# Judging an attention's unshifted exps behind it instead of checking norms in front of it

## The chip, the cores and the metric

The kernel runs on one core of one Trainium2 chip. A core has five engines, each with an instruction queue of its own: TensorE (PE; its weight loads are listed as PEld), VectorE (DVE), ScalarE (ACT), GpSimd (POOL) and SyncE (SP), and 16 DMA engines. The metric is the device time of one execution in microseconds (us): the median of several runs.

## The reference, cut to what matters

Two layers follow each other on 2304 tokens (48 x 48) of 256 channels, all in 32-bit floats. Layer 0 is the one that the change is about: a group norm, three projections, and an attention in which every token contributes 4 rows of 64 channels, so 9216 queries meet 9216 keys.

```python
q = xt @ Wq.T + bq; k = xt @ Wk.T + bk; v = xt @ Wv.T + bv
qf = q.reshape(B * H * W * nh, dk) / jnp.sqrt(jnp.float32(dk))
kf = k.reshape(B * H * W * nh, dk)
vf = v.reshape(B * H * W * nh, dv)
A = jax.nn.softmax(qf @ kf.T, axis=1)
O = A @ vf
out = O.reshape(B, H, W, nh * dv) @ Wo.T + bo      # and x = x + out
```

Layer 1 is an attention over 64 learnt slices of the tokens and a mixture of 8 experts, of which each token uses two.

A softmax is safe in floating point when the largest score of a row is subtracted ahead of the exponential. Without that it gives the same result as long as no sum of exponentials overflows or vanishes. The inputs are normal random numbers, and q and k come from normalised rows and weights of standard deviation 1/16.

## The kernel before, in words

The whole kernel is one function, `tile_conv_attn_hybrid_kernel`, written out as one straight program. A framework (Tile) assigns buffers, inserts semaphores, and orders the instructions of each engine. Instructions issued through `nc.tensor`, `nc.vector` and so on may be reordered by it; those issued through `pe`, `dve`, `act` and `pool` (class `InOrder`, line 55 is what the profile names for all of them) keep the order in which they are written.

**Projections** (lines 235 to 389). After the group norm, a loop over five blocks of tokens (four of 512, one of 256; line 281) makes q and k: for each half m of the channels two matmuls into a PSUM tile `pq` (line 294) and two into `pk` (line 298). Both have the name `pp` and take turns in four buffers of the pool `ps_pj`. From `pq`, VectorE writes three copies and ScalarE one into q2 (lines 312 and 316), from `pk` ScalarE writes kk (line 321).

**The check in front.** Each block also squares q and k on ScalarE (lines 303 and 322), sums the squares per head on TensorE with a matrix `hsel` of zeros and ones (line 328, tile `pn`), and takes maxima on VectorE (line 331). Behind the blocks one transpose (line 338) and a few tiny instructions make `ok`: one if the largest norm of q times the largest norm of k is at most 40, so that no score can be larger than that. Then v follows, 18 tiles of 128 tokens (line 347), again in `pp`, and some folded weights (lines 364 to 389).

**The fork.** `ok` is loaded into a register of each engine (line 674), and `tc.If` (line 677) takes `attention(False)` or, in its Else, `attention(True)`. The latter finds each query's largest score first (`largest`) and adds its negative to the scores by another matmul.

**The attention** (line 503) has 18 blocks of 512 queries; in each a loop over 36 pairs of key tiles. For a pair, `scores` makes 8 score matmuls into `s`, ScalarE takes the exponential into `p` (5 buffers), VectorE adds `p` to `acc` (`sums`), and `times_values` multiplies by v into `av`, one pair behind. The block's end work is spread over the next block: `close` folds `acc` to `both` and `av` to `up`; `between` (at pair 1) sums `both` over the partitions by a matmul of ones into `pb`, and returns a list of small pieces of work: `invert` (reciprocal of the sums), `divide`, and the pieces of `follow`, which runs the output projection, the layer norm and the slice weights of earlier tokens. Each piece has a rank; `in_turn` sorts by it, and one piece is done per pair (`later.pop(0)()`, line 651). In the last block four more rounds of `follow` are drained in the same way (lines 652 to 657). The tiles `pa` and `pb` exist once each.

**Behind the attention** come the last tokens, the slice attention, the gates and the routing. The routing makes 43 slots of 128 token rows, each with one expert (lines 900 to 1030); `slot_t` holds the token numbers, with which GpSimd gathers rows. The loop over the slots (from line 1115) does, for slot s: load slot s + 2, `first(s)` (32 weight loads and matmuls into `ph`, ScalarE's Gelu), and `second(s - 1)` (matmuls into `py`, VectorE's two instructions for `y`, GpSimd's scatter with addition into `t_d`). The last part reads `t_d`, transposes it, and writes the output by SyncE (lines 1132 to 1146). The end of the program (line 1177) waits for the last transfer and clears the semaphores.

Of the kernel before, what the change touches and what calls it, by code (L numbers as in the profile page):

```python
# [14 lines left out]
P = 128  # L15
C = 256
NT = 2304
# [7 lines left out]
NPAIR = NF // (2 * P)  # L25
SAFE = 40.0
S = 64
# [32 lines left out]
@with_exitstack  # L60
def kernel(
    ctx: ExitStack,
    tc: tile.TileContext,
    x, Wq, bq, Wk, bk, Wv, bv, Wo, bo,
    W0, b0, Ws, bs, Wqkv, bqkv, Wout, bout,
    Wg, bg, W1, b1, W2, b2,
    out,
):
    nc = tc.nc
    x_v = x[0].rearrange("(c p) h w -> p c (h w)", p=P)  # L70
# [156 lines left out]
    WoT = l0.tile([P, 2, C], FP, name="WoT")  # L227
    hsel = l0.tile([P, 32], FP, name="hsel")
    hv = hsel.rearrange("p (a b) -> p a b", b=2)
    nc.vector.memset(hsel, 0.0)  # L230
    nc.vector.memset(hv[0:DK, :, 0], 1.0)
    nc.vector.memset(hv[DK:P, :, 1], 1.0)
    ok = l0.tile([1, 1], mybir.dt.int32, name="ok")

    with proj, tc.tile_pool(name="sq", bufs=2) as sqp, tc.tile_pool(
        name="ps_pj", bufs=4, space=PSUM
    ) as ps_pj, tc.tile_pool(name="ps_w", bufs=2, space=PSUM) as ps_w, tc.tile_pool(
        name="ps_n", bufs=1, space=PSUM
    ) as ps_n:
        def transposed(dst, raw):  # L240
# [38 lines left out]

        nmx = pj.tile([P, len(TBLOCKS)], FP, name="nmx")  # L280
        for bi, (t0, tn) in enumerate(TBLOCKS):
            toks = slice(t0, t0 + tn)
            for c in range(2):
# [3 lines left out]
                )  # L287
            sqs = []
            for m in range(2):
                cols = slice(m * P, (m + 1) * P)  # L290
                pq = ps_pj.tile([P, 512], FP, name="pp", tag="pp")
                pk = ps_pj.tile([P, 512], FP, name="pp", tag="pp")
                for c in range(2):
                    nc.tensor.matmul(  # L294
                        pq[:, 0:tn], WqT[:, c, cols], xn[:, c, toks], start=(c == 0), stop=(c == 1)
                    )
                for c in range(2):
                    nc.tensor.matmul(  # L298
                        pk[:, 0:tn], WkT[:, c, cols], xn[:, c, toks], start=(c == 0), stop=(c == 1)
                    )  # L300
                sq = sqp.tile([P, 2, 512], FP, name="sq", tag=f"sq{m}")
                sqs.append(sq)
                nc.scalar.activation(  # L303
                    sq[:, 0, 0:tn], pq[:, 0:tn], AF.Square, bias=bq8[:, m : m + 1], scale=0.125
                )
                for j in range(2):
                    rows = slice(j * DK, (j + 1) * DK)
                    at = (2 * m + j) * NT + t0
                    for half in range(2):
                        dst = q2[half * DK : (half + 1) * DK, at : at + tn]  # L310
                        if j == 1 and half == 1:
                            nc.scalar.activation(
                                dst, pq[rows, 0:tn], AF.Identity, bias=bq8[rows, m : m + 1], scale=0.125
                            )
                        else:
                            nc.vector.tensor_scalar(  # L316
                                dst, pq[rows, 0:tn], bcol[rows, B_Q + m : B_Q + m + 1], 0.125,
                                ALU.add, ALU.mult,
                            )
                bk_m = bcol[:, B_K + m : B_K + m + 1]  # L320
                nc.scalar.activation(kk[:, m, toks], pk[:, 0:tn], AF.Identity, bias=bk_m)
                nc.scalar.activation(sq[:, 1, 0:tn], pk[:, 0:tn], AF.Square, bias=bk_m)

            pn = ps_n.tile([P, 512], FP, name="pn", tag="pn")
            for kind in range(2):
                for m in range(2):
                    r = (2 * kind + m) * 32
                    nc.tensor.matmul(  # L328
                        pn[r : r + 32, 0:tn], hsel, sqs[m][:, kind, 0:tn], start=True, stop=True
                    )  # L330
            nc.vector.tensor_reduce(nmx[:, bi : bi + 1], pn[:, 0:tn], AX.X, ALU.max)
            if bi == 0:
                WvT = transposed(pj.tile([P, 2, C], FP, name="WvT"), raws["Wv"])
                transposed(WoT, raws["Wo"])
        nm = pj.tile([P, 1], FP, name="nm")
        nc.vector.tensor_reduce(nm, nmx, AX.X, ALU.max)
        pr = ps_n.tile([1, P], FP, name="pr", tag="pn")
        nc.tensor.transpose(pr, nm, ident)
        qk2 = pj.tile([1, 2], FP, name="qk2")
        nc.vector.tensor_reduce(qk2, pr.rearrange("p (a b) -> p a b", a=2), AX.X, ALU.max)  # L340
        top = pj.tile([1, 1], FP, name="top")
        nc.vector.tensor_mul(top, qk2[:, 0:1], qk2[:, 1:2])
        nc.vector.tensor_scalar(ok, top, SAFE * SAFE, None, ALU.is_le)
        for i in range(NTT):
# [43 lines left out]
        nc.vector.tensor_copy(bout_bc[:, C : C + E], pw[:, 208:216])  # L388
        nc.vector.tensor_copy(cs_bc, pw[:, 216:224])


# [110 lines left out]

    def attention(shifted):


        with tc.tile_pool(name="pexp", bufs=5) as pexp, tc.tile_pool(
# [107 lines left out]
            def between(b, st):  # L614
# [16 lines left out]

                work.extend([(0, invert), (1, divide)])
                return in_turn(work)
# [4 lines left out]
            for b in range(NQB):  # L638
                row = largest(b) if shifted else None
                st = {}  # L640
                for pair in range(NPAIR):
# [10 lines left out]
                    elif b == NQB - 1 and pair < NPAIR - 1 and drained < 4:  # L652
# [3 lines left out]
                        drained += 1  # L656
                        later.pop(0)()

# [7 lines left out]
            lower()  # L666
            invert, divide = between(NQB - 1, behind)
            invert()
            halves()
            divide()  # L670

    small_scores = nc.values_load(
        ok, min_val=0, max_val=1, skip_runtime_bounds_check_because="it is the result of a comparison"
    )
    with tc.If(small_scores > 0) as fork:
        attention(False)
    with fork.Else():
        attention(True)  # L680

# [219 lines left out]
    with gating, tc.tile_pool(name="onehot", bufs=1) as oh, tc.tile_pool(  # L901
# [125 lines left out]
        dve.tensor_scalar(empties, pw[:, 0, :], 0.0, spare, ALU.is_equal, ALU.mult)  # L1027
        dve.scalar_tensor_tensor(slot_t, pw[:, 0, :], -1.0, empties, ALU.add, ALU.add)
        dve.tensor_copy(slot_w, pw[:, 1, :])
# [7 lines left out]
    with tc.tile_pool(name="ps_h", bufs=3, space=PSUM) as ps_h, tc.tile_pool(  # L1037
        name="ps_y", bufs=2, space=PSUM
    ) as ps_y, tc.tile_pool(name="ps_t", bufs=2, space=PSUM) as ps_t:

# [69 lines left out]
        def turn_next(s):  # L1110
            if s < NSL:
                xs, w1 = loaded.pop(s)
                turned[s] = turn(xs), w1

        turn_next(0)
        for s in range(NSL):
# [3 lines left out]
            if s == 0:  # L1120
                turn_next(1)
            else:
                second(s - 1, hid.pop(s - 1), lambda: turn_next(s + 1))
        second(NSL - 1, hid.pop(NSL - 1), lambda: None)


    with tc.tile_pool(name="fin", bufs=3) as fin, tc.tile_pool(
        name="ps_f", bufs=4, space=PSUM
    ) as ps_f:
        for t0, n in TBLOCKS:  # L1130
# [5 lines left out]
            for c in range(2):  # L1136
# [7 lines left out]
                else:  # L1144
                    nc.scalar.copy(ob[:, c, 0:n], pt[:, 0:n])
            nc.sync.dma_start(out=out_v[:, :, t0 : t0 + n], in_=ob[:, :, 0:n])


# [33 lines left out]
```

## Time and profile before

| what | value |
|---|---|
| median of 3 runs | 1681.72 us (1681.07 to 1682.72) |
| the profiled execution | 1684.09 us |
| its span, first to last instruction | 1682.3 us |
| mean granted clock of TensorE | 0.971 |
| projections, 15.52 to 61.21 us | TensorE busy 45.67 of 45.69 |
| v and folded weights, 61.21 to 79.10 us | TensorE busy 17.89 of 17.89 |
| attention, 79.10 to 1254.70 us | TensorE busy 1170.3 of 1175.6, VectorE 890.87, ScalarE 683.5 |
| slice attention and routing, 1254.7 to 1339.4 us | TensorE busy 56.59 of 84.7 |
| expert slots, 1339.4 to 1656.0 us | TensorE busy 314.99 of 316.6 |
| the rest, 1656.0 to 1682.3 us | TensorE busy 7.51 of 26.3 |

The page of a profile gives, for one execution, the busy time of each engine, the span cut into 40 slices with the busy tenths of each engine and the clock that TensorE was granted, the chain of work that ended last, and the costliest groups of instructions. From the trace behind it one can ask for a timeline, for one tile's or one line's instructions, for the waits, and for a table of busy times by stretch. A matmul of 32-bit floats counts as two instructions. Times within the span are counted from its first instruction.

### The profile page before, as it was taken

What the parts mean: (1) busy time and instruction counts of PE and PEld (TensorE: products, weight loads), DVE (VectorE), ACT (ScalarE), POOL (GpSimd) and SP (SyncE); (2) the same over time, 40 slices, a digit from 0 to 9 for tenths busy, and PEclk for the clock granted to TensorE, in tenths of its full rate; (3) what the DMA queues carried; (4) which work ended last, traced back from release to release, by engine and by line L of the source; (5) the groups of instructions that cost most, each with busy time, mean ns of one, the idle gap of its engine ahead of it and who ended that gap; (6) DMA issues with size and microseconds to landing.
All of it is one profiled execution on the core that took longest, in us unless ns stands there. A gap on an engine that the chain in (4) does not pass through costs nothing.

```text
span 1682.3 us, 32323 instructions
## 1 busy us (share of the span) xinstructions
PE 1617.2 (96%) x13416; PEld 824.3 (49%) x13416; DVE 1039.0 (62%) x1340; ACT 831.7 (49%) x1152; POOL 157.5 (9%) x133
## 2 busy tenths in 40 slices
PE   7999999999999999999999999999987599999995
PEld 3633343333333333333333333333445599999994
DVE  6577777777777777776876877777775511111111
ACT  4355565555655555655655655555542233333331
POOL 0000000000000000000000000000001333333331
PEclk9999999999999999999999999999996599999997
DMA  4000000000000000000000000000007366666664
GB/s 132 1 1 1 1 1 1 1 1 1 1 1 1 1 1 2 1 2 1 2 1 2 2 1 1 1 1 1 1 4 262 135 185 185 188 179 176 183 182 125
DMA packets 41266, 82.91 MB, mean 49 GB/s; under 512 B 3693, under 2 KB 26810, under 8 KB 40986
## 3 DMA queue, kind: packets, MB, share of 16 engines
q1 hardware_dynamic: 32858, 69.49, 12.6%
q0 software_dynamic: 8256, 11.28, 3.9%
q8 instruction: 109, 1.79, 0.5%
q14 instruction: 43, 0.35, 0.1%
HBM read 67.78 MB, written 12.98 MB: 48 GB/s over the span
## 4 chain that ended last, share of the span: by engine, by line
PE 75%; issue 12%; POOL 6%; DVE 3%; DMA 3%; ACT 0%; POOLq 0%; SPq 0%; DVEq 0%; ACTq 0%
PE s L55 33%; PE av L55 33%; POOL t_d L1101 3%; POOL xs L1044 3%; PE pa L55 2%; PE pb L55 1%; DMA t_d<-y,slot_t 1%; PE pp L294 1%; PE pw L55 1%; PE pp L347 1%; PE pp L298 1%; PE pn L328 1%; DMA tt<-t_d 0%; DVE s L55 0%; DMA Wq_raw<-in_L_conv_Wq_dram 0%
## 5 line engine op out<-in xcount | busy, mean ns | idle before, releaser
L55 DVE TENSOR_TENSOR acc<-acc,p 128x1024 f32<-128x1024 f32 x612 | 748.1, 1222 | 270.7 <-ACT p L55 264.2
L55 ACT ACTIVATE p<-s 128x1024 f32<-128x1024 f32 x648 | 663.0, 1023 | 495.8 <-PE s L55 485.7
L55 PE MATMUL av<-p,v_sb 64*64 64x512 f32 x5184 | 676.4, 590 | 1.0 <-DVE up L55 0.7
L55 PE MATMUL s<-q,kk 64*64 64x512 f32 x5184 | 676.0, 590 | 0.0
L55 PEld LDWEIGHTS s<-q,kk 64*64 64x64 f32 x5184 | 202.2, 133 | 351.9 <-issue 180.7
L55 PEld LDWEIGHTS av<-p,v_sb 64*64 64x64 f32 x5184 | 195.9, 131 | 358.0 <-ACT p L55 207.2
L55 ACT ACTIVATE hid<-ph,bcol 128x128 f32<-128x128 f32 x344 | 98.2, 367 | 237.7 <-PE ph L55 198.2
L55 PEld LDWEIGHTS ph<-xT,w 128*128 128x128 f32 x1376 | 163.0, 195 | 3.1 <-DVE xT L55 0.9
L55 PE MATMUL ph<-xT,w 128*128 128x128 f32 x1376 | 163.3, 278 | 0.5 <-DVE xT L55 0.5
L55 PE MATMUL py<-w_sb,hid 128*128 x688 | 162.4, 379 | 0.0
L55 POOL TENSOR_TENSOR rstd_t<-ve,mhalf 128x1 f32<-128x1 f32 (+1 forms) x21 | 28.5, 1356 | 1262.1 <-DVE ve L55 1262.1
L55 DVE COPY xT<-pt 128x256 f32<-128x256 f32 x43 | 18.3, 425 | 186.6 <-PE pt L55 186.6
L55 PEld LDWEIGHTS py<-w_sb,hid 128*128 128x128 f32 x688 | 124.2, 190 | 13.4
L1101 POOL DMA_INDIRECT t_d<-y,slot_t x43 | 68.2, 1585 | 96.2 <-DVE y L55 93.3
L55 DVE TENSOR_TENSOR y<-py,b_bc 128x256 f32<-128x256 f32 x43 | 18.3, 425 | 80.0 <-PE py L55 80.0
L1044 POOL DMA_INDIRECT xs<-tn_d,slot_t x43 | 45.8, 1065 | 120.3 <-PE pt L55 106.9
L55 DVE RECIPROCAL rinv<-pb 128x256 f32<-128x256 f32 x18 | 31.5, 1751 | 0.0
L55 DVE TENSOR_TENSOR acc<-p 128x1024 f32<-128x1024 f32 x18 | 22.1, 1225 | 9.3 <-ACT p L55 9.3
L316 DVE TENSOR_SCALAR q<-pp,bcol 64x512 f32<-64x512 f32 (+1 forms) x30 | 20.8, 694 | 11.2 <-ACT sq L303 10.8
L1139 PE MATMUL pt<-ident,tt 128*128 128x128 f32 x36 | 7.5, 390 | 16.2 <-DMA tt<-t_d 16.2
L55 PE MATMUL pw<-what,t_sb 128*128 128x86 f32 x72 | 15.7, 422 | 6.7 <-POOL what L55 6.7
L55 DVE TENSOR_REDUCE up<-av 128x512 f32<-128x1024 f32 x18 | 21.9, 1217 | 0.0
(252 smaller groups left out, 628.0 us busy)
## 6 DMA issues: line engine op xcount, KB each, us to landing
w<-in_L_ffn_W_dram SPq DMA_DIRECT2D x43, 1024.0 KB
w_sb<-in_L_ffn_W_dram SPq DMA_DIRECT2D x8, 1024.0 KB
x_sb<-in_x_dram SPq DMA_DIRECT2D x4, 576.0 KB
t_d<-t_sb SPq DMA_DIRECT2D x3, 768.0 KB
tn_d<-tn SPq DMA_DIRECT2D x3, 768.0 KB
tt<-t_d SPq DMA_DIRECT2D x4, 512.0 KB
out_dram<-ob SPq DMA_DIRECT2D x4, 512.0 KB
b_bc<-in_L_ffn_b_dram SPq DMA_DIRECT2D x1, 1024.0 KB
```

Source lines behind the costliest of these rows:

```text
L55: return self.tc.keep_in_program_order(getattr(self.engine, name)(*args, **kwargs))
L294: nc.tensor.matmul(pq[:, 0:tn], WqT[:, c, cols], xn[:, c, toks], start=(c == 0), stop=(c == 1))
L298: nc.tensor.matmul(pk[:, 0:tn], WkT[:, c, cols], xn[:, c, toks], start=(c == 0), stop=(c == 1))
L316: nc.vector.tensor_scalar(dst, pq[rows, 0:tn], bcol[rows, B_Q + m : B_Q + m + 1], 0.125, ALU.add, ALU.mult,)
L328: nc.tensor.matmul(pn[r : r + 32, 0:tn], hsel, sqs[m][:, kind, 0:tn], start=True, stop=True)
L347: nc.tensor.matmul(pv[:, 0:C], xn[:, c, i * P : (i + 1) * P], WvT[:, c, :], start=(c == 0), stop=(c == 1),)
L1044: nc.gpsimd.indirect_dma_start(out=xs, out_offset=None, in_=tn_d[:, :], in_offset=bass.IndirectOffsetOnAxis(ap=slot_t[:, s : s + 1], axis= ...
L1101: nc.gpsimd.indirect_dma_start(out=t_d[:, :], out_offset=bass.IndirectOffsetOnAxis(ap=slot_t[:, s : s + 1], axis=0), in_=y, in_offset=None ...
L1139: nc.tensor.transpose(pt[:, k * P : (k + 1) * P], tt[:, k, c * P : (c + 1) * P], ident)
```

## The change

The squares, their sums, the maxima and `ok` are gone, and with them the fork; `ps_pj` has five buffers instead of four. The attention runs without shifted scores. Each block's list gets one more piece, `extremes`, of rank 11: the largest of the partial sums in `both` and the smallest of the whole sums in `pb` go into two columns of `ends_of`. In the last block two pieces instead of one are done at the pair that starts a round of the drain. After slot 3's `second` (at s = 4) `judge` reduces `ends_of` and makes a register-sized `bad`: one if a sum was above 1e20 or below 1e-12; its way goes over a transpose on TensorE into a PSUM bank of its own (`ps_j`). `slot_t` is now clamped to valid rows by one more instruction. The former function is called `layers`; a new function runs it, loads `bad` into a register of each engine, and, under `tc.If`, runs the whole of `layers` again with shifted scores.

```diff
-SAFE = 40.0
+LOW, HIGH = 1e-12, 1e20
...
-    with proj, tc.tile_pool(name="sq", bufs=2) as sqp, tc.tile_pool(
-        name="ps_pj", bufs=4, space=PSUM
-    ) as ps_pj, tc.tile_pool(name="ps_w", bufs=2, space=PSUM) as ps_w, tc.tile_pool(
-        name="ps_n", bufs=1, space=PSUM
-    ) as ps_n:
+    with proj, tc.tile_pool(name="ps_pj", bufs=5, space=PSUM) as ps_pj, tc.tile_pool(
+        name="ps_w", bufs=2, space=PSUM
+    ) as ps_w:
...
-                nc.scalar.activation(
-                    sq[:, 0, 0:tn], pq[:, 0:tn], AF.Square, bias=bq8[:, m : m + 1], scale=0.125
-                )
...
-                nc.scalar.activation(sq[:, 1, 0:tn], pk[:, 0:tn], AF.Square, bias=bk_m)
-
-            pn = ps_n.tile([P, 512], FP, name="pn", tag="pn")
-            for kind in range(2):
-                for m in range(2):
-                    r = (2 * kind + m) * 32
-                    nc.tensor.matmul(
-                        pn[r : r + 32, 0:tn], hsel, sqs[m][:, kind, 0:tn], start=True, stop=True
-                    )
-            nc.vector.tensor_reduce(nmx[:, bi : bi + 1], pn[:, 0:tn], AX.X, ALU.max)
...
+    shifted = bad is None
+    ends_of = const.tile([P, 2, NQB], FP, name="ends_of")
...
-                work.extend([(0, invert), (1, divide)])
+                def extremes():
+                    dve.tensor_reduce(ends_of[:, 0, b : b + 1], st["both"], AX.X, ALU.max)
+                    dve.tensor_reduce(ends_of[:, 1, b : b + 1], pb[:, 256:512], AX.X, ALU.min)
+
+                work.extend([(0, invert), (1, divide), (11, extremes)])
...
                         drained += 1
-                        later.pop(0)()
+                        for _ in later[:2]:
+                            later.pop(0)()
...
-    small_scores = nc.values_load(
-        ok, min_val=0, max_val=1, skip_runtime_bounds_check_because="it is the result of a comparison"
-    )
-    with tc.If(small_scores > 0) as fork:
-        attention(False)
-    with fork.Else():
-        attention(True)
+            extremes()
+
+    attention()
...
-        dve.scalar_tensor_tensor(slot_t, pw[:, 0, :], -1.0, empties, ALU.add, ALU.add)
+        dve.scalar_tensor_tensor(empties, pw[:, 0, :], -1.0, empties, ALU.add, ALU.add)
+        dve.tensor_scalar(slot_t, empties, 0.0, float(NT + P - 1), ALU.max, ALU.min)
...
+        def judge():
+
+            both = fp.tile([P, 2], FP, name="both", tag="judge")
+            for k, op in enumerate((ALU.max, ALU.min)):
+                dve.tensor_reduce(both[:, k : k + 1], ends_of[:, k, :], AX.X, op)
+            dve.tensor_scalar(both[:, 0:1], both[:, 0:1], HIGH, None, ALU.is_gt)
+            dve.tensor_scalar(both[:, 1:2], both[:, 1:2], LOW, None, ALU.is_lt)
+            dve.tensor_tensor(both[:, 0:1], both[:, 0:1], both[:, 1:2], ALU.max)
+            pm = ps_j.tile([1, P], FP, name="pm")
+            pe.transpose(pm, both[:, 0:1], ident)
+            dve.tensor_reduce(bad, pm, AX.X, ALU.max)
...
                 second(s - 1, hid.pop(s - 1), lambda: turn_next(s + 1))
+            if s == 4 and bad is not None:
+                judge()
...
+@with_exitstack
+def tile_conv_attn_hybrid_kernel(ctx: ExitStack, tc: tile.TileContext, *args):
+    verdict = ctx.enter_context(tc.tile_pool(name="verdict", bufs=1))
+    bad = verdict.tile([1, 1], mybir.dt.int32, name="bad")
+    layers(tc, bad, *args)
+    again = tc.nc.values_load(
+        bad, min_val=0, max_val=1, skip_runtime_bounds_check_because="it is the result of a comparison"
+    )
+    with tc.If(again > 0):
+        layers(tc, None, *args)
```

## The prediction

> **What bounds the kernel now.** I read the page's first two parts, then the chain that ended last in order of time, then a table of engine busy time by stage, and last the timelines of the four places that the diff touches. The page (its engine line for TensorE, then the forty slices of TensorE and of its granted clock):
>
> ```profile
> PE 1617.2 (96%) x13416; PEld 824.3 (49%) x13416; DVE 1039.0 (62%) x1340; ACT 831.7 (49%) x1152; POOL 157.5 (9%) x133
> ...
> PE   7999999999999999999999999999987599999995
> ...
> PEclk9999999999999999999999999999996599999997
> ```
>
> TensorE is busy nearly everywhere. The table by stage gives 45.67 of 45.69 us in the projections (15.52 to 61.21), 1170.3 of 1175.6 in the attention (79.10 to 1254.70) and 314.99 of 316.60 in the expert slots (1339.4 to 1656). So an instruction taken from or put on TensorE there counts in full, work on VectorE or ScalarE counts only if TensorE comes to wait for it, and outside these stretches (the end above all) single latencies add up.
>
> **1. The norm check goes: -11.0 us.** One block of 512 tokens in the chain of waits (start, length, engine, tile, line; pp is a projection, pn the sums of squares):
>
> ```profile
> 33.69 0.99 PE pn L328 x6
> 34.67 1.05 PE pp L294 x2
> 35.73 0.98 PE pn L328 x2
> 36.71 1.06 PE pp L294 x2
> 37.76 1.72 PE pp L298 x4
> 39.48 1.72 PE pp L294 x4
> 41.20 1.72 PE pp L298 x4
> 42.91 0.99 PE pn L328 x6
> ```
>
> From pn to pn a block takes 42.91 - 33.69 = 9.22 us. Its four groups of pp take 4 x 1.72 = 6.88 when whole, pn takes 0.99 + 0.98 = 1.97, and the group that pn cuts in two takes 1.05 + 1.06 instead of 1.72. Over the whole chain pn is 4 x 1.97, and 0.56 + 0.55 for the short block: 8.99 us. The cut pieces cost 0.19 once and 0.4 in four more places, two pieces of v (line 347) among them: 1.8. The transpose of the maxima (line 338) is 0.27. Sum 11.06; I write 11.0. The 20 squares on ScalarE (about 12.8 us by line 303's and 322's rows), the 5 reductions (0.69 each) and the memsets of hsel lie beside TensorE and are worth nothing by themselves.
>
> What is late next? In the remaining 34.6 us VectorE needs 29.16 less 3.2 for the reductions = 26 us, ScalarE 25.97 - 12.8 = 13.2. A q tile's PSUM lives 1.72 (matmuls) + 2.29 (three copies on VectorE) + 0.68 (one on ScalarE) + about 0.4 for handovers = 5.1 us; with five buffers and four tiles per 6.88 us a buffer is wanted again after 8.6. TensorE stays the bound, so the 11 us come through.
>
> **2. The fork goes: 0.** Its register loads (0.46 to 0.54 us per engine, line 674) and branches (line 677) lie under running matmuls: TensorE's load is at 77.1, its last small matmul of line 382 ends at 79.19 and the first score matmul follows at once. Behind it the clock is low for a while:
>
> ```profile
> 80.00:82.00 2.00, 2.00 (x16) 0.55 (x12) 0.00 (x0) 1.02 (x1) 0.00 (x0) 0.50 0.02 4
> 82.00:84.00 2.00, 2.00 (x20) 0.72 (x16) 0.69 (x1) 1.02 (x1) 0.00 (x0) 0.69 0.00 0
> ```
>
> (Columns: stretch, length, busy PE, PEld, DVE, ACT, POOL, granted clock, DMA.) In the chain 16 score matmuls take 2.96 instead of 1.72 and 8 value matmuls 1.47 instead of 0.86: 1.85 us lost. The small matmuls of lines 364 to 382 before it stay where they are, so I leave this loss in; if it went with the fork, 1.85 more is won.
>
> **3. Two reductions more per block of the attention: 0.** The maximum over 512 columns is priced like line 331's reduction (0.69), the minimum over 256 like its short form (0.42): 1.1 us, 18 times, 20 in all on VectorE. They have the last rank, so they run after the block's last item, some 15 pairs in. There VectorE has caught up:
>
> ```profile
> 685.21 0.22 DVE L55 TENSOR_TENSOR sw_sum<-sw_sum,sw 128x64 f32<-128x64 f32 x1
> 685.55 1.23 DVE L55 TENSOR_TENSOR acc<-acc,p 128x1024 f32<-128x1024 f32 x1
> 687.27 1.22 DVE L55 TENSOR_TENSOR acc<-acc,p 128x1024 f32<-128x1024 f32 x1 [0.49 <-ACT p L55]
> ```
>
> Each later pair leaves it 0.49 us idle, so 1.1 us is made good in three pairs, and five buffers of p stand between it and ScalarE. Without that cover it is 1.1 us per block. The tile pb is held longer, but the next block wants it some 20 pairs later. Only in the last block does the drain follow at once, and there TensorE first has 1.7 us of out_proj work on pa. The doubled pops move VectorE work by one pair. Behind the loop the last two reductions follow OT at 1254.68, where VectorE idles 3.15 us until the next pm at 1257.84. All of this at 0.
>
> **4. One clamp more for slot_t: +0.2.** A dependent VectorE instruction of 43 columns (its neighbour takes 0.20 with the handover) between the last pw matmul and the gather on POOL; nothing else runs there.
>
> **5. The judge at slot 4: +2.4.** An expert slot where one hands over to the next:
>
> ```profile
> 1361.66 3.73 PE L55 MATMUL ph<-xT,w 128*128 128x128 f32 x32
> 1361.86 0.42 DVE L55 TENSOR_TENSOR y<-py,b_bc 128x256 f32<-128x256 f32 x1 [1.74 <-PE py L55]
> 1362.32 0.35 DVE L55 TENSOR_SCALAR y<-y,slot_w 128x256 f32<-128x256 f32 x1
> ```
>
> Today the next slot's ph matmuls start 0.2 us before VectorE gets to y. All tensor and vector instructions here keep program order, so the judge's transpose stands ahead of those ph matmuls on TensorE, and its five VectorE instructions stand behind y. VectorE is through with y 1.01 us after 1361.66; five dependent small instructions follow at a pitch of 0.2 (the chain of lines 265 to 267: 12.68, 12.87, 13.07), then 0.14 to TensorE and 0.27 for the transpose as at line 338. 1.01 + 1.0 + 0.14 + 0.27 = 2.4. Behind the waiting transpose stand 32 ph matmuls, for which ScalarE waits, then the next slot. Nothing gives it back: every slot is TensorE's for all of its 7.25 us. Below: 2.0, if the two reductions slip in before y is ready. Above: the wait brings the clock down as in the two rows of part 2; with their 1.85 us, 4.25. The Trainium skill, "TensorE: Matmul & The Clock Gate", Part 1, says that the clock falls after an idle window of about 3.4 us; a wait of 2.2 us would then keep it, and the sum would stay at 2.4. The rows show a low clock with less idle time than that, which is why the upper end stays.
>
> **6. The branch at the end: +1.3.** The registers are loaded and the branch is taken over a whole second program, after the last transfer of the output has been issued:
>
> ```profile
> 1679.11 0.37 SPq L1146 DMA_DIRECT2D out_dram<-ob  x1
> ```
>
> SyncE's wait for its landing ends at 1681.4 and the closing drains and semaphores run to 1682.3. So what the branch costs lies beside a landing of 1.9 us. The branch itself, from the old fork (queue, instruction, count, shortest/median/longest in ns, first and last start):
>
> ```profile
> L677 SPq COMPARE_BRANCH  x2: 38/44/49, 62.5 to 62.6; - x2
> ...
> L677 PEldq COMPARE_BRANCH  x2: 95/2013/3931, 77.7 to 1250.9; - x2
> L677 DVEq COMPARE_BRANCH  x2: 51/53/55, 79.9 to 1254.3; - x2
> ```
>
> TensorE's second one, the jump over the Else at 1250.9, lasted 3.93 us, until 1254.83, hidden by the wait for OT (1254.68); the row does not tell a jump from a wait. VectorE's took 0.05. Bounds: with 0.05, SyncE is done at 1679.48 + 0.46 + 0.05 = 1679.99, before the landing: 0. With 3.93, at 1683.9: 2.5 late. If the landing is waited for first: 0.5 + 3.9 = 4.4. I take half of the middle case, 1.3, because TensorE's row is nearest (a jump over a long program) but only one queue shows it. The Trainium skill speaks against the change here: "Runtime: NRT & Kernel Launch", Instruction fetch mechanics, says that a taken branch out of the fetched window stalls until its target's page has been fetched. By that rule every queue would pay something like TensorE's row, and the sum would have 2.5 here instead of 1.3.
>
> **Sum.** -11.0 + 0.2 + 2.4 + 1.3 = -7.1. The profiled execution took 1684.09 with a span of 1682.3; its changed form would be a span of about 1675.2. The runs' median is 1681.72, 2.4 below that execution; differences carry over, so the forecast is 1681.7 - 7.1 = 1674.6.
>
> **Rivals.** (A) The forecast: 1674.6; its own range 1671.0 (-11.0 - 1.85 + 0.2 + 2.0 + 0) to 1678. (B) The costs behind eat the gain: clock down at the judge and the end in series, -11.0 + 0.2 + 4.25 + 4.4 = -2.2: 1679.5. For it the two clock rows and the 3.93; against it the nine other branches of line 677, all under 0.1 us, and the short wait. (C) The projections do not close up: evacuations in series (VectorE's q copies wait for ScalarE's reads of the same tile today, 10.8 us in all) and only half of part 1 comes: -5.5 + 3.9 = -1.6: 1680.1. Against it the 5.1 of 8.6 us above. (D) Slower: the reductions reach TensorE. If VectorE's lag outgrows the five p buffers in each block, 18 x 1.16 = 20.9 come on top: -7.1 + 20.9 = +13.8: 1695.5. It turns the sign by 0.2% from (7.1 + 3.4) / 18 = 0.58 us per block. For it: near the block's start ScalarE already waits for acc, 0.63 us, 16 times. Against it: TensorE does not pause even there, and the last rank comes when 0.49 us per pair is free. (E) The verdict is bad and the second program runs: about twice the time, 3400. Scores of unit variance summed over 9216 keys give thousands, far inside 1e-12 to 1e20.
>
> **Chances.** A 0.70, B 0.15, C 0.08, D 0.06, E 0.01. About 0.2% (3.4 us) is what a measurement here can tell from no change; that is 1678.3. A is faster, B and C are within 0.2%, D and E slower: 0.70, 0.23, 0.07. The range takes all of A and B, 1671 to 1680; C's end and D are left out.
>
> **What would show it.** Right: pp groups back to back from 15.5 to about 47, first score matmul near 68; TensorE's attention stage as long as before (1175.7); one gap of 2.2 us in the fifth slot with the clock at 1.0 behind it; the end later than the landing by 1 to 2 us. Wrong: waits of pp for its buffers; pauses of TensorE once per block; a long branch on SyncE; a second pass.

## The result, and the profile after

The changed kernel takes **1673.86 us** (median of 4 runs, 1672.92 to 1674.74); the kernel before, run beside it, 1682.22 (1681.07 to 1683.55). The ratio is 0.995, with a 95% interval of 0.9933 to 0.9967: faster by 0.5%. Predicted were 1674.6, in a range of 1671 to 1680, and a difference of -7.1; measured is -8.4.

The profiled execution took 1674.74 us with a span of 1672.9, against 1684.09 and 1682.3. First the page's engine line and the two slice rows, which hardly change:

```profile
PE 1603.6 (96%) x13376; PEld 821.5 (49%) x13376; DVE 1051.3 (63%) x1371; ACT 819.3 (49%) x1132; POOL 156.5 (9%) x133
...
PE   7999999999999999999999999999987699999994
...
PEclk9999999999999999999999999999996599999997
```

TensorE lost 40 instructions and 13.6 us, VectorE gained 12.3 us. The sums say little about where the time went; the starts of some TensorE work do. For that, one instruction per stage is looked up in both timelines. A second profile of the kernel before, taken at the end of the study (its execution took 1682.09 us), stands beside the first, because it shows how much two executions of one program differ:

| start of, us | before | before, second profile | after | after less before | after less second |
|---|---|---|---|---|---|
| first score matmul `s` | 79.12 | 79.68 | 68.44 | -10.68 | -11.24 |
| last `pb` from `both` | 1250.87 | 1250.40 | 1239.21 | -11.66 | -11.19 |
| first `pm` behind the attention | 1254.87 | 1253.95 | 1244.19 | -10.68 | -9.76 |
| `pts` | 1267.53 | 1265.87 | 1255.88 | -11.65 | -9.99 |
| first transpose of gathered rows | 1339.45 | 1337.56 | 1327.67 | -11.78 | -9.89 |
| first read of `t_d` (SyncE) | 1660.86 | 1658.87 | 1649.23 | -11.63 | -9.64 |
| last output transfer (SyncE) | 1679.11 | 1677.14 | 1667.27 | -11.84 | -9.87 |
| end of the span | 1682.3 | 1680.4 | 1672.9 | -9.4 | -7.5 |

Read downwards: all of the gain is there when the attention starts, about 1 us is given back between the last `pb` and `pm` (1.4 against the second profile), and 2.4 between the last output transfer and the end. The measured -8.4 lies between the two columns.

**The projections** close up. In the chain of waits of after (start, length, engine, tile, line), the pieces with pn between them are gone:

```profile
35.32 1.72 PE pp L288 x4
37.03 1.72 PE pp L292 x4
38.75 1.72 PE pp L288 x4
```

A block is now four groups of 1.72, 6.88 us, and TensorE never waits for a PSUM buffer there.

**The attention's start.** The scores start 10.7 us earlier, so what was 80 to 84 us before is 69.3 to 73.3 here (stretch, length, busy PE, PEld, DVE, ACT, POOL, granted clock, DMA):

```profile
68.00:70.00 2.00, 2.00 (x21) 0.93 (x20) 0.65 (x5) 0.28 (x1) 0.00 (x0) 1.00 0.00 0
70.00:72.00 2.00, 1.59 (x16) 0.51 (x16) 0.31 (x1) 1.66 (x2) 0.00 (x0) 1.00 0.00 0
72.00:74.00 2.00, 2.00 (x24) 0.73 (x20) 1.05 (x2) 1.02 (x1) 0.00 (x0) 1.00 0.00 0
```

The clock stays at 1.00, where it was 0.50 and 0.69. The 1.85 us are not all won: the faster scores now wait 0.4 us for ScalarE's first exponential. From the first `s` to the last `pb` the attention takes 1170.8 us instead of 1171.75.

**Behind the attention** the timeline of after has this (a bracket: idle time before, and what ended it):

```profile
1242.69 0.42 DVE L55 TENSOR_TENSOR OT<-o,rinv 128x256 f32<-128x256 f32 x1
...
1243.63 0.41 DVE L55 TENSOR_REDUCE ends_of<-pb 128x1 f32<-128x256 f32 x1
1244.19 2.04 PE L55 MATMUL pm<-WoT,OT 128*128 128x256 f32 x4 [4.33 <-DVE ends_of L55]
```

`pm` does not start behind OT (1243.11), but behind the second reduction (1244.04), with which it shares no data.

**The judge** at slot 4, in the same view:

```profile
1361.95 3.62 PE L55 MATMUL py<-w_sb,hid 128*128 x16
...
1365.51 0.16 DVE L55 TENSOR_TENSOR both<-both 128x1 f32<-128x1 f32 x1
1365.72 0.27 PE L55 MATMUL pm<-ident,both 128*1 128x128 f32 x1
```

No bracket stands behind the transpose `pm`: TensorE does not wait at all. The row of `py` has 16 records where a slot shows 10 there: six of the next slot's second layer have moved ahead of the judge's transpose and fill its wait. Over two slots (start of `ph` to start of `ph`) 14.80 us pass instead of 14.50: the judge costs 0.3.

**The end.** First SyncE's waits of before, then of after (who waited for whom: total, times, longest), then the rows of the conditional's line in after (queue, instruction, count, shortest/median/longest in ns, first and last start):

```profile
SPq L1177 <- DMA out_dram<-ob: 1.2, 1, 1.2
```

```profile
SPq L1145 <- SPq L1145: 2.6, 1, 2.6
```

```profile
L1145 SPq EVENT_SEMAPHORE  x9: 17/17/17, 1670.6 to 1671.2; - x9
...
L1145 PEldq COMPARE_BRANCH  x1: 3395/3395/3395, 1666.1 to 1666.1; - x1
...
L1145 SPq COMPARE_BRANCH  x1: 45/45/45, 1668.0 to 1668.0; - x1
```

Compare a queue's branch with its first semaphore. On TensorE the branch itself is recorded with 3.4 us. SyncE's has 0.05 us, at 1668.0, but its next instruction comes at 1670.6. The rows of the other three queues, left out here, are like it: branches of 0.05 to 0.07 us, and the next instruction 2.6 (GpSimd), 2.9 (ScalarE) and 3.0 us (VectorE) after the branch's start. All five queues stall; only one shows it in the branch. SyncE's wait of before, for the transfer's landing, is gone from the list: the stall took its place and ends later.

### The profile page after: what moved, and what is told of

It is laid out like the page before. It is cut to its first block, busy times and chain, and to the rows that moved or that the text cites. A ratio compares the mean times of both kernels' runs of the same rounds, so it can differ in the third digit from the quotient of the medians.

```text
span 1672.9 us, 32258 instructions
## 1 busy us (share of the span) xinstructions
PE 1603.6 (96%) x13376; PEld 821.5 (49%) x13376; DVE 1051.3 (63%) x1371; ACT 819.3 (49%) x1132; POOL 156.5 (9%) x133
## 4 chain that ended last, share of the span: by engine, by line
PE 77%; issue 11%; POOL 6%; DVE 3%; DMA 2%; ACT 0%; POOLq 0%; SPq 0%; ACTq 0%; DVEq 0%
PE s L55 33%; PE av L55 33%; POOL t_d L1075 3%; POOL xs L1018 2%; PE pa L55 2%; PE ph L55 2%; PE pb L55 1%; DMA t_d<-y,slot_t 1%; PE pw L55 1%; PE py L55 1%; PE pp L288 1%; PE pp L292 1%; PE pp L317 1%; DMA tt<-t_d 0%; DVE s L55 0%
## 6 DMA issues: line engine op xcount, KB each, us to landing
w_sb<-in_L_ffn_W_dram SPq DMA_DIRECT2D x8, 1024.0 KB, 10.6
```

## The experiments

Four questions were open: does the clock dip belong to the fork; why does `pm` wait for a reduction; why is the judge free; and what makes the branch slow. Ten kernels were run, in three groups, each group on one chip beside the kernel before (medians 1682.16, 1682.06 and 1682.99).

| run | median, us (lowest to highest) | ratio to before, 95% interval |
|---|---|---|
| after | 1673.86 (1672.92 to 1674.74) | 0.9950 [0.9933, 0.9967] |
| e1_fork_no_check | 1671.10 (1670.27 to 1672.48) | 0.9932 [0.9915, 0.9948] |
| e2_no_branch | 1671.79 (1670.41 to 1672.51) | 0.9935 [0.9919, 0.9952] |
| e7_small_body | 1672.23 (1671.85 to 1674.08) | 0.9944 [0.9927, 0.9960] |
| e4_judge_pinned | 1675.77 (1674.44 to 1676.00) | 0.9958 [0.9944, 0.9972] |
| e6_no_extremes | 1673.36 (1672.17 to 1673.62) | 0.9947 [0.9932, 0.9963] |
| e9_sbuf_extremes | 1672.52 (1671.90 to 1673.91) | 0.9943 [0.9927, 0.9958] |
| e10_fork_ahead | 1673.17 (1672.56 to 1673.82) | 0.9945 [0.9932, 0.9959] |
| e11_fallthrough | 1677.39 (1676.66 to 1677.75) | 0.9967 [0.9955, 0.9979] |
| e5_last_no_pb, e0_before_again | 1672.25, 1682.09 (one run each) | none |

Differences of 1 to 2 us lie inside these intervals; where one is claimed below, it is read from the place in the profile where it arises.

### The check taken out, the fork kept

The kernel before without `pn`, the squares and the maxima; `ok` is a constant, so the fork and its branches stay.

```diff
-            pn = ps_n.tile([P, 512], FP, name="pn", tag="pn")
...
-        nc.vector.tensor_scalar(ok, top, SAFE * SAFE, None, ALU.is_le)
+        nc.vector.tensor_scalar(ok, ones[0:1, 0:1], 2.0, None, ALU.is_le)
```

> The kernel before, with the fork and both attentions, but without the check: no squares, sums of squares or maxima, five buffers for pp, and ok set to one by a single small instruction (so it no longer looks at the norms). Theory 1 (the whole gain is TensorE time of the check): 11.0 us less than before, about 1671.2, the first score matmul near 68.4 us instead of 79.1, and the attention stage as long as before. Rival (the fork itself costs something, at the attention's start or where its Else is jumped over): less than 11 is won here, because the fork stays, and the low clock at the start of the attention stays with it.

1671.10 us, 11.06 less than before: part 1 of the prediction by itself. (The interval leaves some 2.8 us to either side, so the agreement to 0.1 is chance.) The first score matmul comes at 68.56, 10.6 and 11.1 us earlier than in the two profiles of before. The clock behind it (the columns as above):

```profile
70.00:72.00 2.00, 1.56 (x20) 0.51 (x16) 0.11 (x1) 1.80 (x2) 0.00 (x0) 1.00 0.00 0
```

The fork is there, the dip is not, in this stretch as in its neighbours. So the dip does not come with the fork. Whether it came with the check needed the last run.

### The kernel before, profiled again

> The kernel before, unchanged, for a second profile. Theory (the low clock behind the attention's first small matmuls is a matter of when it falls, and not of the fork): the stretch from the first score matmul to the last pb, 1171.7 us in the first profile, may come out anywhere from 1170.6 to 1171.7, with or without a clock below 0.8 between 79 and 84 us; the drain from the last pb to the pts matmul again takes 16.7 us. Rival (the check's small matmuls, which the run without the check lacks, cause it): the same clock of 0.5 to 0.7 at 80 to 84 us and the same 1171.7.

```profile
80.00:82.00 2.00, 1.63 (x16) 0.31 (x8) 0.44 (x5) 1.01 (x2) 0.00 (x0) 1.00 0.00 0
82.00:84.00 2.00, 1.93 (x20) 0.82 (x24) 0.98 (x1) 0.93 (x2) 0.00 (x0) 1.00 0.01 4
```

The same program as in the first profile, check and fork included, and no dip: from the first `s` to the last `pb` 1170.7 us. So the 1 us that the attention seemed to gain is a matter of the execution that was profiled. The rival, that the check's small matmuls bring the dip with them each time, is out too. That they make it likelier is not excluded: in all ten profiles of kernels without the check the clock stays at 1.00 there, and of the two with it one has the dip. The drain (from the last `pb` to `pts`), which the expectation put at 16.7 us again, took 15.5; the fork's branch at its start explains part of that, as the next group shows.

### The reductions behind the attention

First the smallest sum of the last block alone is left out, so that nothing reads `pb` behind the reciprocal.

```diff
+    nc.vector.memset(ends_of[:, 1, NQB - 1 : NQB], 1.0)
...
-                    dve.tensor_reduce(ends_of[:, 1, b : b + 1], pb[:, 256:512], AX.X, ALU.min)
+                    if b < NQB - 1:
+                        dve.tensor_reduce(ends_of[:, 1, b : b + 1], pb[:, 256:512], AX.X, ALU.min)
```

> The changed kernel, but in the last of the 18 blocks the smallest sum is not taken from pb (a one stands in its place, so one block's lower end is not judged). Read from the profile alone: the time from the last sum over partitions (pb) to the first matmul behind the attention (pm), 4.98 us in the changed kernel and 4.00 before. Theory 1 (pm waits for the reader of pb, whose PSUM it takes over): back to 4.0, with pm released by OT. Rival (pm waits for both reductions because they stand behind OT on VectorE): about 4.6, released by the remaining reduction over both.

```profile
1242.22 2.38 PE L55 MATMUL pm<-WoT,OT 128*128 128x256 f32 x4 [2.15 <-DVE rinv L55]
1242.90 0.42 DVE L55 TENSOR_TENSOR OT<-o,rinv 128x256 f32<-128x256 f32 x1
```

`pm` now starts behind the reciprocal, the last reader of `pb`, and 0.7 us ahead of OT. So `pm`'s buffer takes over the PSUM space of `pb`, and its first matmuls read parts of OT that are older than the last block's. From `pb` to `pm` 2.80 us pass instead of 4.98: the late reader costs 2.2 us at the start of `pm`. At the end of this row of `pm` 1.8 are left of it (5.18 us behind the start of `pb` instead of 7.02), because its second half needs OT in any case.

That raises a question about the kernel before, where 4.00 us passed. The answer is the fork. Its jump on TensorE starts right behind `pb`:

| kernel | fork's long branch on TensorE, start + length | `pm` starts | `pb` to `pm` | `pm` to `pts` |
|---|---|---|---|---|
| before | 1250.9 + 3.93 = 1254.8 | 1254.87 | 4.00 | 12.66 |
| before, second profile | 1250.4 + 3.47 = 1253.9 | 1253.95 | 3.55 | 11.92 |
| e1_fork_no_check | 1239.3 + 3.84 = 1243.1 | 1243.18 | 3.91 | 12.67 |
| after | none | 1244.19 | 4.98 | 11.69 |
| e5_last_no_pb | none | 1242.22 | 2.80 | 11.36 |
| e9_sbuf_extremes | none | 1241.10 | 2.80 | 13.17 |

Three times `pm` follows the branch's end within 0.1 us. In the second profile it starts at 1253.95, while OT's last piece, begun at 1253.79, is still being written. The trace named OT as what `pm` waited for in the first profile, but the branch held it. Measured at the start of `pm`, removing the fork therefore was worth 0.8 to 1.2 us in the tail (2.80 against 3.55 to 4.00), and the new reader of `pb` took 2.2 in the same place.

Next, all reductions are left out (`ends_of` is set to one, and the judge finds nothing).

```diff
+    nc.vector.memset(ends_of, 1.0)
...
-                work.extend([(0, invert), (1, divide), (11, extremes)])
+                work.extend([(0, invert), (1, divide)])
...
-            extremes()
```

> The changed kernel without any of the 36 reductions (ends_of is filled with ones at the start, so nothing is judged; the doubled pops stay). Theory 1 (17 of the 18 pairs of reductions lie under TensorE's work, the last one costs 1.0 us behind the attention): the time from the first score matmul to the last pb is the same within 0.3 us (1170.7), and 1.0 us less in all, about 1672.8. Rival (they press on TensorE in each block): the stage from first score to last pb gets shorter by several us, up to 20.

1673.36 us, against 1673.86 of after: not told apart. VectorE's busy time falls from 1051.3 to 1036.2, 15.1 us, and the attention does not move: 1170.9 us from the first `s` to the last `pb`, against 1170.8. The only gain in the profile is the tail's 2.2. Rival D, reductions that reach TensorE, is out. The list of TensorE's waits of after, from 68 to 1250 us, says the same: its only wait for a reduction is the one wait of `pm`; the three other rows add up to 2.3 us.

```profile
PE pm L55 <- DVE ends_of L55: 4.3, 1, 4.3
```

The third takes the largest reciprocal in place of the smallest sum, which judges the same thing and reads SBUF instead of `pb`.

```diff
-                    dve.tensor_reduce(ends_of[:, 1, b : b + 1], pb[:, 256:512], AX.X, ALU.min)
+                    dve.tensor_reduce(ends_of[:, 1, b : b + 1], rinv, AX.X, ALU.max)
...
-            dve.tensor_scalar(both[:, 1:2], both[:, 1:2], LOW, None, ALU.is_lt)
+            dve.tensor_scalar(both[:, 1:2], both[:, 1:2], 1.0 / LOW, None, ALU.is_gt)
```

> The changed kernel with the same judgement taken in another way: instead of the smallest sum in pb (PSUM) the largest reciprocal in rinv (SBUF) is kept, and compared with 1e12. Theory 1 (the last block's wait is for pb's PSUM): pm starts 4.0 us after the last pb instead of 4.98, and the whole is 1.0 us faster than the changed kernel, about 1672.9. Rival (the wait is VectorE's order): no difference.

1672.52 us. The 2.2 us come in `pb` to `pm` (2.80), but the next step, `pm` to `pts`, took 13.17 us in this execution instead of 11.69, and the end of the span is 1671.3. That step is the same work in every kernel of the table, between 11.4 and 13.2 us, and its length goes with the clock behind TensorE's pause: in the 11 us from the start of `pm` the mean granted clock is 0.81 and 0.80 where the step is shortest (e5_last_no_pb, after), 0.78 in the second profile of before, and 0.66 in the three longest. The median is 1.3 us below after's, inside the noise: the mechanism is shown, a faster kernel is not.

### The judge's place on TensorE

What moved the next slot's `py` matmuls ahead of the transpose? The reading put to the test here is this: calls through `pe` keep their order only against the engine's instruction written just before. Ahead of the next slot's `py` that is the load of the expert's number into a register, which is not issued through `pe` and can move. Here this load is written ahead of the judge, so that nothing can pass it.

```diff
+        early = {}
...
-            e = expert_of(s, mybir.EngineType.PE)
+            e = early.pop(s, None)
+            if e is None:
+                e = expert_of(s, mybir.EngineType.PE)
...
             if s == 4 and bad is not None:
+                early[s] = expert_of(s, mybir.EngineType.PE)
                 judge()
```

> The changed kernel with one edit: TensorE's register load of the next slot's expert is issued ahead of the judge, so that the second-layer matmuls behind it are pinned behind the next slot's first layer and cannot float ahead of the judge's transpose. Theory 1 (in the changed kernel six matmul instructions of the next slot fill the wait, so that the judge costs only 0.3 us): here TensorE waits as the prediction worked it out, and the slot is 1.3 to 2.1 us longer than in the changed kernel (the five small instructions turned out to take 0.6 us instead of 1.0). Rival (the judge's wait is short by itself): no difference.

```profile
1361.22 2.32 PE L55 MATMUL py<-w_sb,hid 128*128 x10
...
1364.99 0.27 PE L55 MATMUL pm<-ident,both 128*1 128x128 f32 x1 [1.45 <-DVE both L55]
1365.10 3.73 PE L55 MATMUL ph<-xT,w 128*128 128x128 f32 x32
```

The `py` row is back to 10 records, and TensorE waits 1.45 us for the judge. The next `ph` starts at 1365.10 instead of 1356.13 + 7.25 = 1363.38: 1.72 us, most of it the wait. From the first gathered rows to the first read of `t_d` the slots take 322.95 us, against 321.56 in after: +1.4 = 1.72 - 0.3. The median is 1.9 above after's. So the predicted mechanism exists when the order is held, and the moved matmuls are why it doesn't in the changed kernel. The granted clock stays at 1.00 in all stretches of 2 us from 1358 to 1370.

### The branch at the end

First no load, no conditional and no second program.

```diff
-    again = tc.nc.values_load(
-        bad, min_val=0, max_val=1, skip_runtime_bounds_check_because="it is the result of a comparison"
-    )
-    with tc.If(again > 0):
-        layers(tc, None, *args)
```

> The changed kernel without its second program: the verdict is computed, but no register is loaded from it and nothing is branched over. Theory 1 (the branch over the second program costs what the trace shows between the last output transfer and the end, 5.26 us instead of 2.82): 2.4 us less than the changed kernel, about 1671.4, with the end 2.8 us after the issue of the last transfer. Rival (the value taken in the prediction): 1.3 less, 1672.6. Second rival (the later end is another effect of the run and not of the branch): no difference.

1671.79 us, 2.1 below after. From the issue of the last output transfer to the end of the span 3.5 us pass (1667.11 to 1670.6), against 5.6 in after and 3.2 in before. In SyncE's waits the landing is back, with the same 1.2 us as in before.

Next the same load and branch stay, but over a body of two instructions instead of a whole program.

```diff
     with tc.If(again > 0):
-        layers(tc, None, *args)
+        mark = verdict.tile([1, 8], FP, name="mark")
+        tc.nc.vector.memset(mark, 0.0)
+        tc.nc.sync.dma_start(out=args[-1][0, 0, 47:48, 40:48], in_=mark)
```

> The changed kernel with the same register loads and the same branch at the end, but under the branch stands only one memset and one tiny transfer instead of the second program (the fallback is left out). Theory 1 (the queues stall behind the branch because its target lies far away and must be fetched): the stalls of 2.6 to 3.4 us that each queue shows behind its branch are gone, TensorE's branch takes about 0.1 us, and the time is within 0.5 us of the kernel without any branch. Rival (the stall is the join, its semaphores and the wait for outstanding transfers): the same stall as in the changed kernel, no gain.

```profile
L1145 PEldq COMPARE_BRANCH  x1: 235/235/235, 1665.0 to 1665.0; - x1
...
L1145 SPq COMPARE_BRANCH  x1: 50/50/50, 1666.9 to 1666.9; - x1
L1145 SPq EVENT_SEMAPHORE  x1: 17/17/17, 1667.1 to 1667.1; - x1
```

TensorE's branch takes 0.24 us, and SyncE's semaphore stands 0.2 behind its branch (VectorE's likewise, 1665.8 and 1666.0). The end comes 3.6 us after the last transfer's issue. So load, comparison and branch with a near target cost next to nothing. The join (the semaphore instructions where both paths meet again) is shorter here too, one on SyncE instead of nine; that the 2 us belong to the jump over the long body and not to the join is shown by the last kernel of this group.

Two versions tried to move the stall out of the way. The first puts the conditional ahead of the last part, on top of the kernel with the largest reciprocal, with `ident` and `t_d` shared between both programs.

```diff
     with tc.If(again > 0):
-        layers(tc, None, *args)
+        layers(tc, None, ident, t_d, *args[:-1])
+    last_part(tc, ident, t_d, args[-1])
```

> As the kernel before it, and the branch over the second program is moved ahead of the last part (reading t_d back, transposes, output), which both passes then share. Theory 1 (each queue stalls 2.6 to 3.4 us behind the branch, and at this place TensorE, VectorE, ScalarE and SyncE wait for the last scatter into t_d and its reading anyway): the end is again 2.8 us after the last transfer's issue, 2.4 us less; with the 1.0 us from pb about 1670.5. Rival (SyncE's and GpSimd's joins, which set the semaphores of the part left out and took 0.6 and 1.2 us, now stand ahead of the reading of t_d): the reading starts 0.5 to 2 us later, and about 1672 is left.

1673.17 us. The end is short again (1668.19 to 1671.4, 3.2 us), and TensorE's branch, 3.90 us from 1637.4, lies under the last scatters. But the join of the branch is now in front of the read of `t_d`: GpSimd's join semaphores run from 1645.9 to 1646.8, a semaphore update of 1.2 us follows on the same queue, and the read starts at 1648.24, 5.3 us after the start of the last scatter instead of 3.8 to 3.9. From that read to the last output transfer 19.95 us pass instead of 18.04. The stall is gone and about 3.3 us are lost elsewhere: 1.4 by the join, as the rival said, and 1.9 behind the read, which were not traced.

The second asks the compiler not to lay the body out as the path that falls through, again on top of the kernel with the largest reciprocal.

```diff
-    with tc.If(again > 0):
+    with tc.If(again > 0, preferred_fallthrough_block=False):
```

> This is the run with the maximum of the reciprocals in place of the minimum of pb (1672.5 us), with one more edit: the compiler is asked not to lay the body of the conditional out as the path that falls through. Theory (the stall is the fetch of a far target): the engines take the branch to a near block that holds the join's semaphores, and still jump once over the whole body to the end; the stall moves from in front of the semaphores to behind them, 2.6 to 3.4 us per queue, and the time stays within 1 us of 1672.5. Rival (what is slow is a conditional branch that is decided late, and an unconditional jump is fetched ahead): the stall is gone, and the time falls by about 2.4 us to 1670.

```profile
L1145 SPq EVENT_SEMAPHORE  x9: 17/17/17, 1667.8 to 1670.8; - x9
...
L1145 PEldq COMPARE_BRANCH  x2: 98/1843/3588, 1665.8 to 1666.8; - x2
...
L1145 SPq COMPARE_BRANCH  x2: 38/44/49, 1667.7 to 1670.9; - x2
```

The stall stayed, as the theory said: TensorE's second branch takes 3.59 us. The size was wrong: 1677.39, not within 1 us of 1672.5. SyncE now takes its near branch at 1667.7, waits in the join for the landing until 1670.8, and only then, at 1670.9, takes the far one. Landing and stall stand in series, and from the last transfer's issue to the end 8.5 us pass (1666.98 to 1675.5) instead of 5.8 in the kernel that it was made from (1665.47 to 1671.3). These 2.7 us are the larger part of the 4.2 by which the two spans differ; the other 1.5 lie ahead of the last transfer and were not traced. The second jump leads to the end on every path, though the profile lists it as COMPARE_BRANCH like the first. It is no cheaper, so the rival is out.

## Why the prediction was right, step by step

The forecast was 0.7 us above the median. Three terms were off by 1 us or more, and they cancel: the judge cost 2.1 less, the branch 1.1 more, the handover behind the attention 1.0 to 1.4 more. The main term, the check, was right; that the sum came within 1 us is luck. The sum so mended is -6.7 against the second profile of before, which differs by -7.5, and -7.1 against the first, which differs by -9.4. Of the 2.3 left there, 1.9 are the attention's start and the step from `pm` to `pts`, both at a lower clock in that execution. The 0.8 left to the second is spread over several rows of the table.

- **1. The norm check, -11.0: right.** With the check alone removed -11.06, and 10.6 and 11.1 us at the first score matmul, by the two profiles of before. The buffers, of which five were counted as enough, held TensorE nowhere. Four were not tried.
- **2. The fork, 0, and the clock: wrong in two places.** The jump of 3.93 us at 1250.9 was taken as "hidden by the wait for OT". It was not: `pm` started at its end in three profiles, and without it would have started 0.8 to 1.2 us earlier. And the dip of the clock, left in by the forecast, is not a property of the program; it came in one of two profiles of the kernel before.
- **3. The reductions, 0: right for 17 blocks, wrong for the last.** The working looked for an idle VectorE and found 3.15 us, but did not ask which PSUM space the next `pm` gets. It gets that of `pb`, whose last reader had moved from the reciprocal to the reduction: 2.2 us. With the 0.8 to 1.2 us that the fork gave back, the tail is 1.0 to 1.4 us later, not 0.
- **4. The clamp, +0.2: right.** From `pw` to the first gathered rows 19.96 us instead of 19.79.
- **5. The judge, +2.4: too high by 2.1.** The failed step is "All tensor and vector instructions here keep program order". Register loads do not, and the `py` matmuls behind one moved with it. Held in order, the judge costs 1.72, still less than 2.4. The 1.01 us until VectorE is through with `y` came as foreseen (1364.39 - 1363.38); from there to the transpose 0.60 pass instead of 1.14, because the first reduction begins before `y` ends and the others follow in 0.1 to 0.2; and the transpose holds up the next `ph` by 0.11 instead of 0.27.
- **6. The branch, +1.3: too low by 1.1.** The half of 2.5 was taken because "only one queue shows it". Every queue stalls; four of them show it only as a gap in front of the next instruction. Measured: 2.4 from the ends, 2.1 from the medians without a branch. Here the Trainium skill, "Runtime: NRT & Kernel Launch", Instruction fetch mechanics, had said it right: a taken branch out of the fetched window waits for its target's page, and the sum by that rule (2.5) was the better one. The small body, with the same branch and a near target, fits it.

Rival B (1679.5) failed at both of its conditions: no lower clock at the judge, and the end is not in series. The fall-through version shows what the series costs. Rival C did not occur: the projections close up to 6.88 us a block. D was tested and is out. E did not occur: the program ran once.

What stays open: the cause of the low clock. It falls in the drain too, by different amounts in executions of the same work, and the runs only show that neither the fork nor the check brings it each time at the attention's start.

## What to carry to other kernels

A buffer that gets one more reader is handed on later, so ask who takes the space over, even if the new reader's engine is idle. A jump over a long body stalled every queue here, even where the branch's record is short: look at the gap in front of the next instruction, and place the jump where the queue has something else to wait for. The fork behind the attention had that in part, the end of the program did not. And before an order of instructions is put into a sum, look for the ones that are free to move.

## What the runs showed of the hardware

- **The far jump.** In after, 2.6 to 3.0 us between a recorded branch of 0.05 to 0.07 us and the next instruction on SyncE, GpSimd, ScalarE and VectorE (2.5 to 3.4 in the other kernels with this jump; 5.2 on SyncE where the conditional stands ahead of the last part), and 3.4 to 3.9 us in TensorE's own record over all kernels. With a near target it is 0.2 us on SyncE and VectorE, and 0.24 us in TensorE's record.
- **The landing beside it.** Where the far jump follows the last output transfer, that transfer lands 2.9 to 3.7 us after its issue; without a branch, with the small body, with the conditional ahead, and in the kernels with the old fork it is 2.1 us, wherever the profile gives it. Why was not looked into.
- **The clock behind short pauses.** In the kernel without the last `pb` reduction TensorE pauses 0.89 us, works 0.65 and pauses 2.15; then the clock is down:

```profile
1242.20:1244.20 2.00, 1.98 (x4) 1.24 (x5) 1.67 (x4) 0.00 (x0) 0.00 (x0) 0.50 0.00 0
```

  Behind the judge's single wait of 1.45 us it stayed at 1.00. The Trainium skill, "TensorE: Matmul & The Clock Gate", Part 1, puts the fall behind an idle window of about 3.4 us. No single pause in this stretch is that long, and the clock fell all the same. In after, in the pause of 4.33 us from 1239.86 on, it averages 0.67 from 1241 to 1243, so it fell less than 3.2 us into the pause. The measurement decides: the length of one pause alone does not foretell the clock. What else does was not tried.
